# First sequence's weighted values summed by TensorE in PSUM, with new ranks for the first phase's order

## The chip, the cores and the metric

One Trainium2 chip, one core of it. The metric is the device time of one execution in microseconds (us), the median over several runs.

## What is computed

Two transformer-like layers over 32 sequences of 256 tokens, 256 wide, 16 heads of 16. The first step of the first layer is what the change is about: each token's projected vector `kx` is cut into 16 heads, and the heads of one token attend to each other.

```python
kx = modulated_linear(x, s, k_aff_w, k_aff_b, k_w, k_b)
kx = kx.reshape(B, N, H, D)                                   # 32, 256, 16, 16
q = k = v = kx
scores = jnp.einsum('bnhd,bnjd->bnhj', q, k) / math.sqrt(D)   # heads by heads, within a token
A = jax.nn.softmax(scores, axis=-1)
out = jnp.einsum('bnhj,bnjd->bnhd', A, v).reshape(B, N, F)    # weighted values
out = modulated_linear(out, s, o_aff_w, o_aff_b, o_w, o_b)
...
x = x + _L0_attn_ref(_L0_cond_ref(x, ...), ...)               # attention over tokens, cosine scores
x = x + _L0_ffn_ref(_L0_cond2_ref(x, ...), ...)               # adapter, second attention, mixture of experts
x = x + _L1_attn_ref(...); x = x + _L1_ffn_ref(...)           # second layer
```

## The kernel before

Tokens lie on the 128 partitions, so a sequence is two tiles (`t` = 0, 1) of 128 tokens by 256 values. The kernel has three phases. The first takes every sequence from its input to the router's logits of the mixture of experts; the second runs the experts; the third runs the second layer. Only the first phase is changed. It ends, in the profiled execution, with the last scores' sums on TensorE at 1622 us and the last logits at about 1633 us.

The order of the first phase's instructions is written by a planner that runs when the kernel is built (`side_by_side`, line 98). Each of the 32 sequences is a Python generator (`sequence`, line 1142) that says before each step which engine it wants and for how long the planner should reckon with it (`yield DVE, 0.7`), and then issues its instructions. At each turn the planner takes the step that can start first; among equals the lower rank goes first. The rank is the sequence's number plus a number for the stage that it is in: the table `STAGES`. A low rank of "in", for instance, lets new sequences start early. Engines then run their instructions strictly in the planned order, each waiting for its own inputs on the chip. "DVE2" is a VectorE (DVE) step that the planner keeps off GpSimd's (POOL's) time, and PER, PEC and PEH are TensorE (PE) steps in other tile modes, with a small charge for the change of mode.

Buffers are rings with turns: a generator asks for one (`get("hp", ...)`), and gives it back (`back("hp")`). The ring "hp" has three buffers of 128 x 2048 values; "mm" has three banks of PSUM; seven sequences may be under way (`lanes`).

`head_softmax_attention` (line 747) does the attention between heads of a token, on DVE, because it is a small product for each token. `kk` holds each token's 256 values twice, side by side. For the scores, DVE multiplies `kk` with shifted copies of itself (L775) and sums over the 16 values of a head (L780); ScalarE (ACT) takes the exponentials (L805 to L808); DVE sums them and takes the reciprocals (L816 to L819, into `rs`). The answers follow: for each tile `t` and each half `j0` of the 16 shifts, DVE forms 8 weighted copies (L827, 128 x 2048), then halves them three times by adding one half to the other (L835: 1024, 512 and 256 values); the two halves are added (L837) and multiplied with the reciprocals (L839). The result `o0` goes to PE, which transposes it (L292) and projects it (L304); from there come `x0T` and the queries, keys and values (L866, L312), whose norms need GpSimd's power (L262) and a product on DVE (L856) before PE can transpose them (L890) and form scores (L1019). ACT takes the exponentials (L1028), PE forms the weighted sums (L1001) and transposes them (L1049), and DVE divides (L1056, `o_n`).

A second copy of the phase, with an exact softmax, stands behind a branch and is taken only if the first pass finds sums out of bounds; with these inputs it is not.

Of the kernel before, what the change touches and what calls it, by code (L numbers as in the profile page):

```python
# [17 lines left out]
ALU = mybir.AluOpType  # L18
# [4 lines left out]
P = 128  # L23
S = 256
D = 256
H = 16
DH = 16
# [5 lines left out]
PE, DVE, ACT, POOL, SP = "PE", "DVE", "ACT", "POOL", "SP"  # L33
DMA = "DMA"
DVE2 = "DVE2"
# [62 lines left out]
def side_by_side(parts, lags):  # L98
# [84 lines left out]


STAGES = {
    "in": 1.0,
    "heads": 0.5,
    "answers of heads": 1.0,
    "out of heads": 0.0,
    "queries": 0.0,  # L190
    "queries by token": 0.0,
    "scores 1": -1.5,
    "tokens 1": 0.0,
    "out 1": -6.0,
    "x1": -0.5,
    "adapter": -2.5,
    "norm 1": 2.5,
    "queries 2": 0.0,
    "scores 2": -0.5,
    "tokens 2": 5.5,  # L200
    "out 2": 0.0,
    "norm 2": -0.5,
    "gates": -0.5,
    "values": -0.5,
    "norms of queries": 0.0,
    "answers": 1.0,
    "tokens": -4.5,
    "residual in": 0.0,
    "adapter's weights": 5.5,
    "bias": 0.5,  # L210
    "residual out": 0.0,
}


# [1 line left out]
def network(ctx: ExitStack, tc: tile.TileContext, a: dict, out: bass.AP):  # L216
    nc = tc.nc
# [19 lines left out]
    ident = cst.tile([P, P], F, name="ident")  # L237
# [86 lines left out]
    def get(r, name, shape=None, dtype=F):  # L324

        pool, own, turns = rings[r]
        yield turns
        return pool.tile(shape or own, dtype, name=name, tag=r)

    def back(r):  # L330
        return "back", rings[r][2]
# [47 lines left out]
    def condition_tables(l, w, style, demod, d2, n, at=0.0):  # L379

        yield None, at
        own = w is None
        if own:
            w = yield from get("sh", "w")
        aff = yield from get("sh", "aff", [P, D])
        yield SP, 0.5
        nc.sync.dma_start(aff, a[l + "affT"])
        yield SP, 0.5
        nc.sync.dma_start(w, a[l + "wT"].rearrange("(k p) n -> p k n", p=P))
        yield None, 3.0  # L390
        w2 = yield from get("sh", "w2")
        s2 = sm.tile([P, 2, B], F, name="s2")
        ps = yield from get("mm", "mm", [P, 2, B])
        yield PE, 0.8
        for m in range(2):
            nc.tensor.matmul(ps[:, m, :], aff[:, m * P : (m + 1) * P], condT, start=True, stop=True)
        yield ACT, 0.5
        for m in range(2):
            nc.scalar.activation(
                style[:, m, :], ps[:, m, :], AF.Identity, bias=col(l + "aff", m),  # L400
                scale=1.0 / math.sqrt(P) if l == "c" else 1.0,
            )
        yield back("mm")
        yield DVE, 0.9
        nc.vector.tensor_mul(w2, w, w)
        nc.vector.tensor_mul(s2, style, style)
        ps = yield from get("mm", "mm", [P, 2, B])
        yield PE, 1.8
        for m in range(2):
            for c in range(2):  # L410
                nc.tensor.matmul(
                    ps[:, m, :], w2[:, c, m * P : (m + 1) * P], s2[:, c, :], start=(c == 0), stop=(c == 1)
                )
        yield DVE, 0.25
        nc.vector.tensor_copy(d2, ps.rearrange("p m b -> p b m"))
        yield back("mm")
        yield back("sh")
        yield back("sh")
        if own:
            yield back("sh")  # L420
        yield from demodulation(demod, d2, 0, n)
# [45 lines left out]
    before = cst.tile([P, NSB, NT * NE], BF, name="before")  # L467
# [274 lines left out]
    def windows(kk, j0, n):  # L742

        v = kk[:, :, j0 * DH : j0 * DH + D]
        return bass.AP(v.tensor, v.offset, [v.ap[0], v.ap[1], (DH, n), (1, D)])

    def head_softmax_attention(kk, o0, b, exact):
# [21 lines left out]
        for j0 in range(0, 9, 4):  # L769
            n = min(4, 9 - j0)  # L770
            r = "hp" if n == 4 else "sh"
            w = D if n == 4 or exact else D // 2
            pr = yield from get(r, "hprod", [P, 2, n, w])
# [35 lines left out]
        rs = rhead[:, 2 * b : 2 * b + 2, :]  # L809
# [3 lines left out]
        else:  # L813
# [3 lines left out]
            nc.vector.tensor_reduce(rs2, weights(0, 8, 8, 2).rearrange("p t j h -> p t h j"), AX.X, ALU.add)  # L817
            nc.vector.tensor_add(rs, rs, rs2)
        nc.vector.reciprocal(rs, rs)  # L819
        yield "stage", "answers of heads"  # L820
        for t in range(2):
            prs = []
            for j0 in (0, 8):
                pr = yield from get("hp", "hprod2")
# [317 lines left out]
    def sequence(b, exact):  # L1142
# [8 lines left out]
        yield None, 2.5  # L1151
        yield "join", tables[b >= N0, "k"]
        yield ACT, 0.95
# [22 lines left out]
        yield "stage", "heads"  # L1176
        o0 = yield from get("sh", "o0")
        yield from head_softmax_attention(kk, o0, b, exact)
        yield back("kk")
        yield "stage", "out of heads"  # L1180
# [6 lines left out]
        yield back("sh")  # L1187
        yield "join", tables[b >= N0, "o"]
        yield "join", constants_part
# [119 lines left out]
        yield "back", lanes  # L1309

    N0 = min(B, 4)
    tables = {}
    for l in ("k", "o", "c"):
        d2 = wA.tile([P, B, 2], F, name="d2_" + l)
        n = B if l == "c" else N0
        tables[False, l] = Part(condition_tables(l, wT.get(l), sty[l], dem[l], d2, n, 300.0 if l == "c" else 0.0))
# [1123 lines left out]
```

## Time and profile before

| | |
|---|---|
| median of 3 runs | 3713.29 us (3712.82 to 3715.05) |
| profiled execution, its own time | 3708.21 us |
| its span, first to last instruction | 3706.5 us |
| mean granted TensorE clock | 0.978 |
| PE busy | 3488.0 us (94%) |
| DVE busy | 2467.3 us (67%) |
| ACT busy | 1805.9 us (49%) |
| POOL busy | 1887.7 us (51%) |

In the lines of the timeline the columns are start, duration, engine, line of the kernel, operation, output<-input, shapes, the number of instructions merged, and in brackets the engine's idle time before and what ended it. A float32 matmul appears as two records. Matmul durations overlap by a little, so sums of single records can exceed the stretch in which they ran.

### The profile page before, as it was taken

To read this page: it belongs to the slowest core of one execution; us is meant where nothing else is said; L and a number is where in the kernel's file an instruction comes from. 1 tells how busy PE (TensorE), PEld (TensorE's weight loads), DVE (VectorE), ACT (ScalarE), POOL (GpSimd) and SP (SyncE) were. 2 spreads that over 40 slices of the span, in tenths; PEclk is the share of its full clock that TensorE was granted. 3 is DMA by queue.
4 is the path that set the end of the run, shared out by engine and by line. 5 is a ranking of instruction groups with operands and counts; after the bars stand their busy time and mean duration, and the time that the engine had idled before them with its cause. 6 is when DMAs were issued, how large, how long until landed. Compare 5 with 4: busy or idle time off the path is not lost. (4 is left out here: it accounts for less than half of the span.)

```text
span 3706.5 us, 55576 instructions
## 1 busy us (share of the span) xinstructions
PE 3488.0 (94%) x22001; PEld 2564.0 (69%) x22001; DVE 2467.3 (67%) x4039; ACT 1805.9 (49%) x2790; POOL 1887.7 (51%) x1515
## 2 busy tenths in 40 slices
PE   3899999999999999969999999999998999999999
PEld 2566666666666666646666666666787888888888
DVE  7999999999999999747654540011346656565554
ACT  2677777777777777732222222222333333333333
POOL 4546555555555554426546665553024656565553
PEclk7999999999999999979999999999999999999999
DMA  1011010100100111032334334222341323233321
GB/s 64 16 34 33 31 31 31 31 31 27 29 25 28 31 31 37 25 123 69 101 83 106 97 76 91 44 37 40 131 168 43 105 93 116 94 97 97 120 94 43
DMA packets 136495, 241.44 MB, mean 65 GB/s; under 512 B 19265, under 2 KB 80897, under 8 KB 133666
## 3 DMA queue, kind: packets, MB, share of 16 engines
q0 software_dynamic: 48128, 100.77, 11.2%
q1 hardware_dynamic: 87954, 136.51, 11.1%
q8 instruction: 176, 2.88, 0.3%
q14 instruction: 93, 0.76, 0.1%
q10 hardware_dynamic: 144, 0.52, 0.0%
HBM read 187.25 MB, written 50.48 MB: 64 GB/s over the span
## 5 line engine op out<-in xcount | busy, mean ns | idle before, releaser
L1028 ACT ACTIVATE pt<-sc 128x2048 f32<-128x2048 f32 x256 | 481.5, 1881 | 108.6 <-PE sc L1019 105.7
L1633 ACT ACTIVATE hid<-bh,cols 128x512 f32<-128x512 f32 x256 | 175.3, 688 | 600.5 <-PE bh L1644 600.5
L1659 PE MATMUL by<-w,hid 128*128 128x256 f32 x2048 | 454.5, 380 | 3.2 <-DVE ysb L1665 3.2
L1644 PE MATMUL bh<-ehT,w 128*128 128x512 f32 x1024 | 451.5, 594 | 0.8 <-DVE ysb L1665 0.8
L1659 PEld LDWEIGHTS by<-w,hid 128*128 128x128 f32 x2048 | 387.7, 191 | 67.8 <-issue 14.3
L262 POOL TENSOR_TENSOR n<-n,negh 128x32 f32<-128x32 f32 x64 | 364.8, 5700 | 5.3
L1567 POOL DMA_INDIRECT rrows<-ysb,row x128 | 220.3, 1721 | 259.7 <-DMA rrows<-ysb,row 146.2
L1665 DVE TENSOR_TENSOR ysb<-by,b 128x512 f32<-128x512 f32 x64 | 44.0, 688 | 456.9 <-PE by L1659 382.7
L1644 PEld LDWEIGHTS bh<-ehT,w 128*128 128x128 f32 x1024 | 194.8, 191 | 220.8 <-issue 214.7
L256 POOL TENSOR_SCALAR rstd<-mv 128x2 f32<-128x2 f32 x160 | 62.7, 392 | 506.9 <-DVE mv L362 500.5
L835 DVE TENSOR_TENSOR hprod<-hprod 128x1024 f32<-128x1024 f32 (+2 forms) x384 | 313.3, 816 | 7.1
L1019 PE MATMUL sc<-qT,kT 32*128 32x256 f32 x4096 | 294.2, 401 | 19.4 <-ACT pt L1028 17.8
L827 DVE TENSOR_TENSOR hprod<-hex,kk 128x2048 f32<-128x2048 f32 x128 | 292.2, 2283 | 0.0
L1001 PE MATMUL av<-pt,vaug 128*32 128x256 f32 x4096 | 271.8, 385 | 5.6 <-ACT pt L1028 5.6
L1019 PEld LDWEIGHTS sc<-qT,kT 32*128 32x128 f32 x4096 | 185.4, 184 | 93.7 <-ACT pt L1028 42.7
L2269 PE MATMUL dh<-zT,w_eff 128*128 128x256 f32 x1024 | 235.9, 379 | 0.5 <-DVE zT L2246 0.5
L2283 PE MATMUL do<-w_con,gT 128*128 128x256 f32 x1024 | 230.9, 379 | 0.0
L1600 POOL DMA_INDIRECT xg<-h2buf,tok x128 | 149.3, 1167 | 156.8 <-issue 69.1
L256 POOL TENSOR_SCALAR n<-n 128x32 f32<-128x32 f32 x64 | 57.1, 892 | 300.7 <-DVE n L877 184.7
L2283 PEld LDWEIGHTS do<-w_con,gT 128*128 128x128 f32 x1024 | 192.0, 190 | 24.7
L2269 PEld LDWEIGHTS dh<-zT,w_eff 128*128 128x128 f32 x1024 | 189.9, 190 | 24.2 <-ACT cT_s L344 0.7
L1001 PEld LDWEIGHTS av<-pt,vaug 128*32 128x32 f32 x4096 | 108.0, 109 | 121.0 <-issue 54.1
(615 smaller groups left out, 7375.3 us busy)
## 6 DMA issues: line engine op xcount, KB each, us to landing
w<-in_w SPq DMA_DIRECT2D x16, 1024.0 KB, 8.2
x<-rrows SPq DMA_DIRECT2D x64, 256.0 KB, 3.1
bfw<-in_upw SPq DMA_DIRECT2D x10, 1024.0 KB, 6.9
bfw<-in_dnw SPq DMA_DIRECT2D x10, 1024.0 KB, 5.1
xT<-in_xT SPq DMA_DIRECT2D x32, 256.0 KB, 3.5
x<-in_x SPq DMA_DIRECT2D x32, 256.0 KB, 2.8
ugbb<-gtab SPq DMA_DIRECT2D x32, 256.0 KB, 3.8
h2buf<-xh SPq DMA_DIRECT2D x32, 256.0 KB, 2.5
```

The lines of the kernel that those rows point to most:

```text
L262: nc.gpsimd.tensor_tensor(o, o, negh[:p].to_broadcast([p, n]), ALU.pow)
L827: nc.vector.tensor_tensor(pr.rearrange("p j (h d) -> p j h d", d=DH), weights(t, j0, 8)[:, 0].unsqueeze(3).to_broadcast([P, 8, H, DH]), wi ...
L835: nc.vector.tensor_tensor(pr[:, :n], pr[:, :n], pr[:, n : 2 * n], ALU.add)
L1001: nc.tensor.matmul(av[32 * i : 32 * i + 32, c % 2, :], va[:, kc, 4 * c + i, :], pt[:, i, kc, :], start=(kc == 0), stop=(kc == 1),)
L1019: nc.tensor.matmul(sc[:, i, kc, :], kT[r, m, kc * P : (kc + 1) * P], qT[r, e, m, :], start=True, stop=nm is None,)
L1028: nc.scalar.activation(pt, sc, AF.Exp, scale=1.0 / math.sqrt(DH))
L1567: nc.gpsimd.indirect_dma_start(rrows[:, :], bass.IndirectOffsetOnAxis(ap=row[:, j0 + t : j0 + t + 1], axis=0), y[:, t, :], None, compute_o ...
L1633: nc.scalar.activation(o, ps, AF.Relu, bias=bcol)
L1644: nc.tensor.matmul(ps, w["w1"][:, c, f * P : (f + 1) * P], hT[c], start=(c == 0), stop=(c == 1))
L1659: nc.tensor.matmul(ps[:, t, :], hid[f // 4][:, f % 4, (t0 + t) * P : (t0 + t + 1) * P], w["w2"][:, f, :], start=(f == 0), stop=(f == 7),)
L2269: nc.tensor.matmul(ps[:, g, :], w_eff[:, c, f * P : (f + 1) * P], zT[:, c, :], start=(c == 0), stop=(c == 1))
L2283: nc.tensor.matmul(ps[:, t, :], gT[:, f, t * P : (t + 1) * P], w_con[:, f, :], start=(f == 0), stop=(f == 7))
```

## The change

For the first `NPE` = 1 sequences, in the pass that is not exact, the three halvings, the last addition and the product with the reciprocals are replaced. DVE still forms the four weighted products of 128 x 2048. PE then multiplies each of their 8 parts (128 x 256) with the identity matrix and accumulates the 16 parts of a tile in PSUM. DVE takes the sums of both tiles from PSUM in one instruction that multiplies with the reciprocals. The sums of one product run as a part of their own (`summed`), each behind the one before it, and give the "hp" buffer back. All later sequences are done as before, but the ranks in `STAGES` are other ones, so the order of all sequences' instructions on every engine differs. In the changed kernel L827, L835, L837 and L839 of the later sequences are L860, L868, L870 and L872.

```diff
 STAGES = {
-    "in": 1.0,
-    "heads": 0.5,
-    "answers of heads": 1.0,
-    "out of heads": 0.0,
-    "queries": 0.0,
+    "in": -5.5,
+    "heads": 0.0,
+    "answers of heads": 0.0,
+    "out of heads": -0.5,
+    "queries": -2.0,
     "queries by token": 0.0,
-    "scores 1": -1.5,
-    "tokens 1": 0.0,
-    "out 1": -6.0,
-    "x1": -0.5,
-    "adapter": -2.5,
-    "norm 1": 2.5,
-    "queries 2": 0.0,
-    "scores 2": -0.5,
-    "tokens 2": 5.5,
-    "out 2": 0.0,
-    "norm 2": -0.5,
-    "gates": -0.5,
-    "values": -0.5,
-    "norms of queries": 0.0,
+    "scores 1": 1.0,
+    "tokens 1": 1.0,
+    "out 1": -1.5,
+    "x1": 0.0,
+    "adapter": -4.0,
+    "norm 1": 3.0,
+    "queries 2": 4.0,
+    "scores 2": -1.0,
+    "tokens 2": 4.0,
+    "out 2": -3.0,
+    "norm 2": 0.0,
+    "gates": 0.0,
+    "values": 0.0,
+    "norms of queries": -0.5,
     "answers": 1.0,
-    "tokens": -4.5,
-    "residual in": 0.0,
-    "adapter's weights": 5.5,
-    "bias": 0.5,
-    "residual out": 0.0,
+    "tokens": -2.5,
+    "residual in": 7.0,
+    "adapter's weights": 6.0,
+    "bias": 0.0,
+    "residual out": 2.0,
 }
...
         nc.vector.reciprocal(rs, rs)
+        if not exact and b < NPE:
+
+            ps = yield from get("mm", "mm", [P, 2, D])
+
+            def summed(pr, t, j0, before):
+                if before is not None:
+                    yield "join", before
+                yield PE, 3.45
+                for n in range(8):
+                    nc.tensor.matmul(ps[:, t, :], ident, pr[:, n], start=(j0 + n == 0), stop=(j0 + n == 15))
+                yield back("hp")
+
+            last = None
+            for t in range(2):
+                for j0 in (0, 8):
+                    pr = yield from get("hp", "hprod2")
+                    yield DVE2, 2.3
+                    nc.vector.tensor_tensor(
+                        pr.rearrange("p j (h d) -> p j h d", d=DH),
+                        weights(t, j0, 8)[:, 0].unsqueeze(3).to_broadcast([P, 8, H, DH]),
+                        windows(kk, j0, 8)[:, t].rearrange("p j (h d) -> p j h d", d=DH),
+                        ALU.mult,
+                    )
+                    last = Part(summed(pr, t, j0, last))
+                    yield last
+            yield "join", last
+            yield DVE, 0.7
+            nc.vector.tensor_tensor(
+                o0.rearrange("p t (h d) -> p (t h) d", d=DH), ps.rearrange("p t (h d) -> p (t h) d", d=DH),
+                rs.rearrange("p t h -> p (t h)").unsqueeze(2).to_broadcast([P, 2 * H, DH]), ALU.mult,
+            )
+            yield back("mm")
+            return
         yield "stage", "answers of heads"
...
     N0 = min(B, 4)
+    NPE = 1
```

## The prediction

> **What bounds the kernel now.** First the page's slices, to see where which engine is short of work. Each digit covers 92.7 us.
>
> ```profile
> ## 2 busy tenths in 40 slices
> PE   3899999999999999969999999999998999999999
> DVE  7999999999999999747654540011346656565554
> PEclk7999999999999999979999999999999999999999
> ```
>
> TensorE (PE) is nearly full from the third slice to the end; only the first slice, and the gap at slice 18 where the first phase ends, are thin. VectorE (DVE) is as full as PE, but only in the first 16 slices. The change touches only that first phase, so I cut it into stretches (columns: stretch, its length, busy time of PE, weight loads, DVE, ACT, POOL, then the granted clock).
>
> ```profile
> 0.00:44.00 44.00, 16.14 (x64) 12.91 (x64) 25.19 (x29) 12.07 (x27) 26.02 (x22) 0.82 0.40 129
> 44.00:100.00 56.00, 21.67 (x72) 15.21 (x76) 53.23 (x66) 14.06 (x29) 11.95 (x4) 0.59 0.04 11
> 100.00:200.00 100.00, 83.97 (x717) 54.76 (x713) 90.89 (x131) 66.92 (x101) 49.00 (x27) 0.95 0.05 15
> 200.00:1500.00 1300.00, 1248.67 (x11252) 847.62 (x11252) 1239.01 (x1856) 1000.80 (x1486) 695.86 (x427) 1.00 0.10 31
> 1500.00:1622.00 122.00, 116.26 (x1115) 77.86 (x1112) 73.13 (x158) 89.53 (x115) 34.81 (x32) 1.00 0.08 24
> ```
>
> At 1622 us the last score work of the phase is done. PE idles 27.9 + 34.3 + 16.0 + 51.3 + 5.7 = 135.2 us on the way and works 1486.7. DVE idles only 2.8 us in 44 to 100 and 61 us in 200 to 1500. So the start is DVE's, the tail after 1500 is PE's, and in between neither leads clearly. The waits of PE in the first 200 us name the culprit of the start (columns: total, times, longest):
>
> ```profile
> PE mm L292 <- DVE o L839: 38.2, 3, 27.6
> PE mm L890 <- DVE qk L856: 17.1, 3, 9.0
> ```
>
> L839 is the last step of the first sequence's answers. The timeline shows what DVE does before it, and what PE does after it:
>
> ```profile
> 41.53 2.28 DVE L827 TENSOR_TENSOR hprod<-hex,kk 128x2048 f32<-128x2048 f32 x1
> 43.85 2.41 DVE L835 TENSOR_TENSOR hprod<-hprod 128x1024 f32<-128x1024 f32 x3
> ...
> 61.15 0.43 DVE L837 TENSOR_TENSOR o<-hprod,hprod 128x256 f32<-128x256 f32 x1
> 61.61 0.42 DVE L839 TENSOR_TENSOR o<-o,rall 128x256 f32<-128x256 f32 x1
> 63.56 3.78 PE L304 MATMUL mm<-o0T,w_owT 128*128 128x256 f32 x8 [0.56 <-ACT o0T L348]
> ```
>
> Four products of 2.28 us, each followed by three halvings (2.41 us), and two pairs of small steps (0.85 us): 20.5 us, in which PE has nothing.
>
> **The change, part by part.**
>
> *DVE's relief.* Removed: 4 x 2.41 + 2 x 0.85 = 11.3 us. Added: one eviction of 128x512 from PSUM with the reciprocal; its nearest row is L1284, the same shape out of PSUM, 0.69 us. Net 10.6 us off DVE, all within a stretch in which DVE has no slack.
>
> *PE's sums.* 32 products of 128x256. The row "PE do L2283 x16" of the chain (two records to a product) takes 3.45 us for 8 such products, so 13.8 us at full clock. They start at 43.9, after 20 us without PE work, and there the trace has the clock at 0.50: from 63.56, PE ran without a gap, and the clock stayed at 0.50 until about 69.2, 5.6 us. With 5.6 us at half speed the sums take 13.8 + 2.8 = 16.6 us; the ends are 13.8 (no cold time) and 27.6 (all cold). I take 16.6, since the sums are a gapless run like that at 63.56.
> [...]
>
> *Hand-offs.* The "hp" ring has three buffers. In the new order DVE makes pieces 1 and 2 (43.8, 46.1), then a small score group and one full product of sequence 2 that keeps the third buffer (49.3), then pieces 3 and 4. Piece 3 therefore waits for PE's first sum (8 products, 5.6 us cold and the rest warm: until 50.2), piece 4 for the second (53.6). What is queued behind them on DVE is the row sum, the first product and first halving of sequence 2; all of it slips by these two waits, 0.9 and 1.1 us. PE's fourth sum ends at 60.5, DVE is at its eviction at 60.9, and o0 is complete at 61.6: only 0.4 us before today's 62.03. The first sequence hardly gains; what gains is that DVE has by then done 8.6 us (10.6 - 2.0) of other work. Bounds: 10.6 if the ring never holds DVE, and 0 if PE stays cold (its fourth sum then ends at 71.5, DVE waits some 10 us).
>
> *Warm clock.* The transposes and the two projections behind o0 took 1.34, 3.78 and 2.78 us cold; the transposes in a warm row take 0.60 (L292 at 1497.69), the projections 1.89 each (L304 at 19.37). If PE stays warm: 3.5 us less work. Bounds 0 and 3.5; I take 3.5.
>
> *PE's idle time in 44 to 100.* Adding DVE's rows along the new order from 61.6: sequence 2's o0 is complete at 81.4, and the first sequence's second normalized queries at 91.7, against 92.5 now. PE idles about 0.5 in the sums, 2.5 at eviction and o0T, 10.4 while it waits for sequence 2's o0 (71 to 81.4), 2 in that chain, 2 before the queries' transposes and 1 after: 18.4 in place of 34.3.
>
> *The new ranks.* They move everything: the order of nearly every later instruction differs. Two counts from the order: DVE's work ahead of the last o0 falls by 17.7 us (11 of them the relief, the rest small steps put behind it, where DVE has 49 us free); and PE's work behind the last o0 grows. Before, that o0 is done at 1496.2 and PE has 119.5 us of work in the 125.8 us to 1622. The new order has there 24 more score products (24.1 us for 168: 3.4), 24 more weighted sums (3.2), 8 + 8 + 4 more projections (3.9 + 4.0 + 1.9), 24 more transposes (3.8) and 4 router products (1.0): 21 us more, so the phase ends 147 us behind the last o0.
> Activation table loads (65) and changes of PE's tile mode (916) are the same in both orders: no charge.
>
> *The sum.* PE's account: work 1486.7 + 13.8 + 2.8 - 3.5 = 1499.8; idle 27.9 + 18.4 + 16.0 + 51.3 + 5.7 = 119.3, with everything from 100 us on as now. End at 1619.1, 2.9 us earlier. DVE's account: last o0 at 1496.2 - 17.7 + 2.0 = 1480.5 if DVE idles as much as now, plus 147: 1627.5, 5.5 us later. The two contradict each other by 8.4 us: at 1480.5 PE would idle some 10 us more in the steady part than now, or, if PE idles as now, DVE some 10 us less. For DVE idling less speaks that the order has its heads some 20 us of PE work further ahead: its waits for PE, ACT and POOL in 200 to 1500, 37 us by name, have more to hide behind, and PE's 16 us of idle in 100 to 200 should shrink with sequence 2 ready 14 us sooner (I take a fifth, 3 us). So I follow PE's account, and take 5 us earlier than now: 0.15%. Behind 1622 nothing changes.
>
> The profiled execution took 3708.21 us (span 3706.5 and 1.7 around it), 5.1 below the median of 3713.29; the change carries over to the median: **3708**.
>
> **The rivals.**
>
> *A, a small gain, as summed:* -5 us, itself between -12 and +1 by the bounds above. For it: the start is DVE's with certainty. Against it: the first sequence itself hardly gains. 0.40.
>
> *B, the new order also closes waits in the steady part.* PE's named waits there are 49 us, the largest for o_n (L292, 16.7), the exponentials (L1019, 12.5) and x (L292, 8.9). A third less gives 16 more: -21, 3692. For it: the ranks were set for another beginning and the whole order is new. Against: PE is 96% busy there, and each of these waits is a chain inside one sequence. 0.20.
>
> *C, slower: the tail behind the heads decides.* If DVE keeps its idle time of now, or loses more (the ring waits recur, PE's sums stay cold), the 21 us of PE work put behind the last o0 aren't paid for. Price: +5.5 at today's DVE idle, and one more for each us that DVE idles more; at 10 more, +15, 3729. It decides as soon as DVE's waits do not shrink by 5.5 us. For it: in 1500 to 1622 PE is 95% busy, so work moved there counts in full. 0.25.
>
> *D, no effect:* DVE's lead runs into the same waits of both engines and the end stays within 2 us: 3713. For it: both engines idle 4 to 5% in the steady part, each on the other. 0.15.
>
> **How the numbers follow.** About 0.2% (7.4 us) is what a measurement of this kernel can tell from no change. Faster by more: all of B and two fifths of A (its part beyond -7.4), 0.36. Slower by more: C with 2 us or more of added DVE idle, 0.22, and 0.03 of D: 0.25. Within: 0.24 of A, 0.03 of C and 0.12 of D, 0.39. The range from 3693 to 3724 holds A and D, the nearer half of B, and C up to 5 us of added DVE idle.
>
> **What would show it.** Right: four groups of 8 matmuls from about 44 to 61, the first at clock 0.5; o0 of the first sequence at 61 to 62; o0 of the second at about 81, where it is now at 95; last o0 between 1465 and 1481; end of the scores between 1610 and 1623. Wrong: the clock stays at 0.5 through the sums, DVE waits over 4 us for "hp", or PE's idle time in 200 to 1500 moves by more than 10 us from 51, in either direction: then the ranks, and not the sums, set the result.

## The result, and the profile after

The changed kernel takes 3731.51 us (median of 5 runs, 3727.24 to 3733.99), the kernel before 3713.38 us (5 runs, 3712.82 to 3715.82) on the same chip: a ratio of 1.0047, with a 95% interval from 1.0037 to 1.0058. It is 18 us slower, where 5 us faster was forecast. The profiled execution took 3733.99 us, its span is 3731.9.

The page's slices look almost alike (each digit is now 93.3 us). PE's row has the same digits from slice 3 to slice 28, with the gap at the end of the first phase still in slice 18; only DVE's digits around it differ (5, 5, 6 in slices 17 to 19, where they were 7, 4, 7):

```profile
## 2 busy tenths in 40 slices
PE   5799999999999999969999999999888999999999
...
DVE  7999999999999999556664541001336656565554
...
PEclk8899999999999999989999999999999999999999
```

The stretches show more. Columns as before: the first pair is PE, the third pair DVE, and the number ahead of the last two is the granted clock.

```profile
0.00:44.00 44.00, 15.88 (x65) 12.81 (x66) 25.27 (x29) 12.47 (x28) 26.03 (x22) 0.81 0.40 129
44.00:100.00 56.00, 43.74 (x184) 32.73 (x188) 50.91 (x64) 23.58 (x44) 19.17 (x6) 0.88 0.05 16
100.00:200.00 100.00, 75.49 (x595) 48.54 (x591) 89.97 (x119) 55.68 (x83) 44.77 (x24) 0.86 0.05 15
200.00:1500.00 1300.00, 1244.11 (x11130) 844.39 (x11129) 1221.63 (x1834) 991.84 (x1465) 694.07 (x427) 0.99 0.09 30
1500.00:1622.00 122.00, 119.98 (x1134) 83.46 (x1133) 73.89 (x163) 93.47 (x124) 34.75 (x33) 1.00 0.08 24
1622.00:1645.00 23.00, 18.55 (x185) 11.92 (x183) 6.06 (x18) 11.06 (x12) 2.17 (x3) 1.00 0.07 25
```

The start went as promised: from 44 to 100 PE works 43.7 us in place of 21.7, at clock 0.88 in place of 0.59. Then it turns: from 100 to 200 PE does 8.5 us less than before, and the clock is 0.86 where it was 0.95. From 200 to 1500 the clock reads 0.99 and not 1.00. That looks like rounding, but it stands for 34.1 us at half clock, as is shown below.

The timeline of the start, PE and DVE:

```profile
43.77 16.01 PE L829 MATMUL mm<-hprod,ident 128*128 128x256 f32 x64 [19.64 <-DVE hprod L837]
...
49.46 2.29 DVE L837 TENSOR_TENSOR hprod<-hex,kk 128x2048 f32<-128x2048 f32 x1 [0.59 <-PE mm L829]
52.91 2.29 DVE L837 TENSOR_TENSOR hprod<-hex,kk 128x2048 f32<-128x2048 f32 x1 [1.16 <-PE mm L829]
...
59.99 0.68 DVE L847 TENSOR_TENSOR o<-mm,rall 128x512 f32<-128x512 f32 x1
```

The sums, the two waits for "hp" (0.59 and 1.16 us) and the eviction (0.68 us) stand where the prediction put them, to within 1 us.

A good mark for the end of the first phase is the small product of `okmin` behind the last scores. Its row (the two times are its first and last start), before and after:

```profile
L1350 PE MATMUL mm<-okmin,ones x2: 167/168/168, 1622.0 to 1622.0; 128*1 128x5 f32 x2
```

```profile
L1384 PE MATMUL mm<-okmin,ones x2: 166/166/167, 1642.6 to 1642.6; 128*1 128x5 f32 x2
```

So 20.6 us are lost inside the first phase. The waits of PE in the first 200 us, and then in 200 to 1500:

```profile
PE mm L829 <- DVE hprod L837: 19.6, 1, 19.6
PE mm L923 <- DVE qk L889: 13.1, 4, 5.5
```

```profile
PE mm L292 <- DVE o L872: 26.0, 17, 3.0
PE mm L312 <- DVE o_n L1089: 12.5, 12, 1.1
```

Before, the wait of the o0 transposes for DVE cost 0.2 us in all of 200 to 1500, and no steady wait of PE was longer than 1.9 us:

```profile
PE mm L292 <- DVE x L1224: 8.9, 12, 1.9
...
PE mm L292 <- DVE o L839: 0.2, 1, 0.2
```

Now there are 17 waits of the o0 transposes, up to 3.0 us; seven of PE's waits there are 2.4 us or longer. One of them, with PE and DVE side by side:

```profile
500.64 2.41 DVE L868 TENSOR_TENSOR hprod<-hprod 128x1024 f32<-128x1024 f32 x3
501.29 0.33 PE L292 MATMUL mm<-ident,o 128*128 128x128 f32 x1
503.08 0.43 DVE L870 TENSOR_TENSOR o<-hprod,hprod 128x256 f32<-128x256 f32 x1
503.54 0.42 DVE L872 TENSOR_TENSOR o<-o,rall 128x256 f32<-128x256 f32 x1
...
504.02 0.55 PE L292 MATMUL mm<-ident,o 128*128 128x128 f32 x3 [2.40 <-DVE o L872]
...
505.15 2.09 PE L1052 MATMUL sc<-qT,kT 32*128 32x256 f32 x16
```

PE has transposed the first token tile of o0 and waits while DVE halves and scales the second. The score products behind it take 2.09 us; the same 16 records took 1.15 us at 499.21. The stretches say why:

```profile
502.00:504.00 2.00, 0.00 (x0) 0.00 (x0) 1.90 (x5) 2.00 (x4) 0.00 (x0) 1.00 0.00 0
504.00:505.00 1.00, 0.98 (x7) 0.76 (x7) 1.00 (x3) 0.45 (x3) 0.30 (x1) 1.00 0.00 0
505.00:506.00 1.00, 1.00 (x11) 0.78 (x12) 1.00 (x2) 0.45 (x2) 0.97 (x1) 0.57 0.08 16
506.00:508.00 2.00, 2.00 (x20) 0.83 (x20) 2.00 (x2) 0.64 (x1) 0.00 (x0) 0.50 0.00 0
508.00:509.00 1.00, 1.00 (x14) 0.38 (x7) 1.00 (x1) 1.00 (x1) 0.00 (x0) 0.73 0.00 0
```

A wait of 2.40 us, and behind it 3.4 us at half clock. The trace's clock has eight such stretches from 200 to 1500 us, 34.1 us together; before, it has none there.

To weigh this I summed PE's time of the first phase in half-microsecond stretches: busy time times clock is work at full clock, busy time times (1 - clock) is what the slow clock cost, the rest is idle. (Work is good to some 5 us, by my estimate: of the 13.8 us of the sums only 7.5 show up.)

| first phase, us | end | work | idle | slow clock |
|---|---|---|---|---|
| before | 1622.0 | 1476.9 | 135.2 | 9.9 |
| after | 1642.6 | 1484.4 | 127.0 | 31.6 |

The difference is +7.5 work, -8.2 idle, +21.7 slow clock. By this account the clock took everything. The experiments had to say whether that is so.

### The profile page after: what moved, and what is told of

Its sections match the earlier page's. It is cut to its first block, busy times and chain, and to the rows that moved or that the text cites. A ratio compares the mean times of both kernels' runs of the same rounds, so it can differ in the third digit from the quotient of the medians.

```text
span 3731.9 us, 55605 instructions
## 1 busy us (share of the span) xinstructions
PE 3516.1 (94%) x22065; PEld 2589.2 (69%) x22065; DVE 2452.8 (66%) x4024; ACT 1810.2 (49%) x2790; POOL 1884.8 (51%) x1515
## 5 line engine op out<-in xcount | busy, mean ns | idle before, releaser
L262 POOL TENSOR_TENSOR n<-n,negh 128x32 f32<-128x32 f32 x64 | 354.3, 5536 | 5.3
L868 DVE TENSOR_TENSOR hprod<-hprod 128x1024 f32<-128x1024 f32 x372 | 328.8, 884 | 8.0
L1052 PE MATMUL sc<-qT,kT 32*128 32x256 f32 x4096 | 302.2, 410 | 17.1 <-ACT pt L1061 14.5
L860 DVE TENSOR_TENSOR hprod<-hex,kk 128x2048 f32<-128x2048 f32 x124 | 293.7, 2368 | 0.0
L256 POOL TENSOR_SCALAR n<-n 128x32 f32<-128x32 f32 x64 | 39.2, 612 | 458.2 <-DVE n L910 456.5
L2317 PEld LDWEIGHTS do<-w_con,gT 128*128 128x128 f32 x1024 | 192.3, 190 | 24.5
L780 DVE TENSOR_REDUCE hex<-hprod 128x64 f32<-128x1024 f32 (+1 forms) x192 | 166.9, 902 | 1.8
```

What stands on the lines that cost most here:

```text
L262: nc.gpsimd.tensor_tensor(o, o, negh[:p].to_broadcast([p, n]), ALU.pow)
L860: nc.vector.tensor_tensor(pr.rearrange("p j (h d) -> p j h d", d=DH), weights(t, j0, 8)[:, 0].unsqueeze(3).to_broadcast([P, 8, H, DH]), wi ...
L868: nc.vector.tensor_tensor(pr[:, :n], pr[:, :n], pr[:, n : 2 * n], ALU.add)
L1052: nc.tensor.matmul(sc[:, i, kc, :], kT[r, m, kc * P : (kc + 1) * P], qT[r, e, m, :], start=True, stop=nm is None,)
L2317: nc.tensor.matmul(ps[:, t, :], gT[:, f, t * P : (t + 1) * P], w_con[:, f, :], start=(f == 0), stop=(f == 7))
```

## The experiments

All ratios are to the kernel before on the same chip, 95% intervals in brackets.

**1. The parts alone.** The theory was that the new ranks are at fault, the rival that the sums are. First the ranks of before with the sums:

```
-    "in": -5.5, ...        # all of STAGES as in the kernel after
+    "in": 1.0, ...         # all of STAGES as in the kernel before; NPE = 1 stays
```

> The change with the ranks of before: the first sequence's sums on TensorE alone. Theory (the new ranks are at fault: TensorE meets waits of 2.4 us and more in the steady part, its clock halves after them): no such waits, no halved clock between 200 and 1480 us, and a time from 9 us below the kernel before to 3 us above it (3704 to 3716). Rival (the sums are at fault, 13.8 us of work put on an engine that bounds the phase): 8 to 15 us above the kernel before.

Measured: 3812.29 us, ratio 1.0287 [1.0273, 1.0301]. And the new ranks without the sums (`NPE = 0`):

> The new ranks without the sums: all sequences on VectorE as before. Theory (the ranks are at fault): slower than the kernel before by 15 to 30 us, with halved clock in the steady part as in the changed kernel. Rival (the sums are at fault): within 6 us of the kernel before.

Measured: 3830.61 us, ratio 1.0330 [1.0316, 1.0344]. Theory and rival both miss by far, and in the same direction. From 200 to 1500 us, first of the one and then of the other:

```profile
200.00:1500.00 1300.00, 1186.32 (x10291) 798.67 (x10294) 1170.15 (x1721) 924.96 (x1381) 639.57 (x393) 0.97 0.09 28
```

```profile
200.00:1500.00 1300.00, 1201.44 (x10535) 810.19 (x10536) 1178.10 (x1730) 942.32 (x1404) 652.44 (x400) 0.97 0.09 28
```

PE idles 114 and 99 us there in place of 51, with 16 and 18 half-clock stretches (72 and 89 us). So neither part can be priced by taking the other out: in both runs the planner wrote another order for all 32 sequences, with new waits and half-clock stretches in it. Parts have to be compared in a fixed order.

**2. The clock alone, in the order of after.** The theory now: waits of 2.4 us and more in the steady part, and the half clock behind them. Eight products of the identity with itself, which nobody reads, are put ahead of the o0 transposes of six sequences, at which PE waited 2.4 to 3.0 us (0.216 us each, an estimate: in before's trace products of twice the width follow each other after 0.432). The seventh long wait, the one that ends at 313.97, is left as it was:

```
+    WARM = {b: 8 for b in (8, 10, 14, 18, 22, 26)}
...
+        for _ in range(warm):
+            nc.tensor.matmul(ps[:, 0, :P], ident, ident, start=True, stop=True)
         transpose2(ps, x2)
```

> The changed kernel with 8 more identity products (128 columns, 1.7 us together, results overwritten) ahead of the transposes of o0 in the six sequences 8, 10, 14, 18, 22 and 26, where TensorE waits 2.4 to 3.0 us: TensorE works in the wait, and what remains of it is 0.7 to 1.3 us. Theory (the wait lets the clock halve for 3.4 or 6.8 us behind it): no halved clock at those six places, 7 to 15 us faster than the changed kernel. Rival (only the waits themselves cost): same time as the changed kernel within 3 us, or slower by up to 10 us, since 10 us of work are added.

Measured: 3716.54 us, ratio 1.0025 [1.0015, 1.0035]: 8 us faster than after (by the ratios 0.22%) with 10 us more of PE work. Its stretch, the waits at these transposes, and the end of the phase:

```profile
200.00:1500.00 1300.00, 1253.98 (x11313) 855.36 (x11312) 1225.10 (x1844) 999.92 (x1475) 693.58 (x427) 1.00 0.10 30
```

```profile
PE mm L292 <- DVE o L876: 15.0, 17, 1.2
```

```profile
L1390 PE MATMUL mm<-okmin,ones x2: 167/167/167, 1631.6 to 1631.6; 128*1 128x5 f32 x2
```

The clock is at 1.00, the six waits are 1.2 us or shorter, and the phase ends 11.0 us sooner. Two half-clock stretches are left (6.8 us), and one of them stands behind the wait that was left as it was (2.78 us, ending at 313.06; half clock from 313.7 to 317.1). ACT's exponentials of the scores, 256 in all, show that this is the steady part's doing: the 65th, 97th, 129th, 161st and 193rd come 14.5, 14.4, 16.0, 18.7 and 21.4 us later in after than in before, but 10.4, 10.3, 10.3, 10.3 and 10.3 us later in after_filled. At full clock the new order runs as fast as the old one there; it is behind from the beginning.

**3. A rank against those waits.** If they come from the place of the transposes, a later rank for them should help:

```
-    "out of heads": -0.5,
+    "out of heads": 0.5,
```

> The changed kernel with one rank changed, that of the stage out of heads from -0.5 to 0.5, so that TensorE's transposes of o0 come later in its order. Theory (the waits at these transposes and the clock behind them are the loss): fewer waits over 2 us and a time nearer to the kernel before, 5 to 20 us faster than the changed kernel. Rival (the loss is the longer tail behind the last heads): no faster than the changed kernel by more than 4 us unless the last o0 moves.

Measured: 3771.38 us, ratio 1.0169 [1.0155, 1.0183], 14 half-clock stretches. A miss: as in experiment 1, the planner wrote another order for everything.

**4. The sums alone, in the order of after.** Instructions in after's order, but the first sequence's products are halved by DVE, and the identity products are left out (the 17.7 us in the expectation are the prediction's count of all DVE work that leaves the stretch ahead of the last o0; the sums' own part is 10.6):

```
-                for n in range(8):
-                    nc.tensor.matmul(ps[:, t, :], ident, pr[:, n], ...)
+                    for n in (4, 2):
+                        nc.vector.tensor_tensor(pr[:, :n], pr[:, :n], pr[:, n : 2 * n], ALU.add)
```

> The order of instructions of the kernel after, on every engine, with one difference: the first sequence's four products are summed by VectorE's halvings again and TensorE's 64 identity products are left out; the whole computation is done. It prices the sums alone, inside the new order. Forecast's term: the halvings take some 17.7 us more of VectorE than the sums leave it (with 2 us for the scaled eviction), so if VectorE's relief at the beginning carries to the end of the first phase: 8 to 16 us slower than after (3731.5), that is 3739 to 3748. Rival (the relief is absorbed by waits later in the phase, because TensorE's late stages, and not VectorE's sum, end the phase): within 4 us of after, 3727 to 3736. Second rival (the clock: starting later shifts the half-clock stretches): anything up to 15 us either way, with a different number of half-clock stretches between 200 and 1500 us than after's 8.

Measured: 3742.47 us, ratio 1.0077 [1.0063, 1.0091].

```profile
L1389 PE MATMUL mm<-okmin,ones x2: 167/168/168, 1651.2 to 1651.2; 128*1 128x5 f32 x2
```

The phase ends 8.6 us after that of after, and the exponentials are 10.5 us late at the first and 8.5 to 8.6 from the 65th on. The clock is not the reason: it costs 30.1 us here, in seven steady half-clock stretches, against 31.6 in eight. Here DVE's relief does reach the end: 8.6 us at the mark, where the prediction's net relief was 8.6 (10.6 less 2.0 for the ring). That they agree to the tenth is chance, but the size is right.

**5. The sums in the order of before.** before's order is written out as a list and followed; the first sequence is summed by PE, and its eviction is set behind DVE's next steps for the second and third sequences, so that DVE doesn't wait for it. In a second version the other sequences stand 8 us earlier against the first.

```
-    side_by_side(parts, lags)
+    side_by_side(parts, lags, listed=ORDER)   # before's order, step by step
+    NPE = 1
```

> The kernel before with its order of steps written out as a list and followed, but the first sequence's four products summed by TensorE, and VectorE's scaled eviction set behind the next two or three VectorE steps of the second and third sequences, so that it doesn't wait. No ranks are used, nothing else moves. Theory (the sums are worth having, and what made the kernel after slower is the new order with its TensorE waits of 2.4 us and more and the half-clock stretches behind them): no more than 2 half-clock stretches in 200 to 1500 us, the second sequence's o0 10 to 15 us earlier, and a time 2 to 12 us under before, 3696 to 3706. Rival (the relief at the beginning is absorbed, since the same order waits for the same later steps): within 2 us of before, 3706 to 3710. Second rival (the small shift breaks the timing of the steady part as any change of ranks did): 10 us slower or more, with 5 or more half-clock stretches.

> As the run before it (before's order as a list, the first sequence's sums on TensorE, the eviction set back), but in the list all steps of the other sequences stand 8 us (of the plan's time) earlier against the first sequence's, for the time that the sums set free. Theory: as the run before it or better, 3692 to 3706, no more than 2 half-clock stretches in 200 to 1500 us. Rival (the relief is absorbed): 3706 to 3710. Second rival (shifting the sequences against each other makes new waits of 2.4 us and more on TensorE): slower by 10 us or more, with 5 or more half-clock stretches.

Measured: 3711.20 us, ratio 0.9997 [0.9988, 1.0006], and 3729.42 us, ratio 1.0046 [1.0032, 1.0059]. In the first, the exponentials start 4.1 us sooner than before's, and from the 21st on they are 0.3 to 2.3 us ahead, with a half-clock stretch at 236 us that before hasn't. Most of the relief is gone at once: DVE stands still for the first sequence's gate, which comes from PE and stands ahead of DVE's next halvings in this order.

```profile
70.55 0.16 DVE L1215 SCALAR_TENSOR_TENSOR gate<-mm,cols 128x2 f32<-128x2 f32 x1 [6.56 <-PE mm L1213]
```

In the second they are 12.7 us late by the ninth, with seven half-clock stretches in the first 200 us and two behind. The first rival holds for the one. The second rival's price holds for the other, though its half-clock stretches lie mostly ahead of the steady part: the relief is worth little in before's order, and shifting the sequences by hand costs as much as the change did.

**6. The cold start of before.** Its PE waits in the first 135 us filled with unread products (246 in all):

```
+        for _ in range(warm):          # 165 ahead of o0's transposes, 40 and 27
+            nc.tensor.matmul(...)      # among the queries', 14 ahead of x1's
```

> The kernel before, order and ranks unchanged, with identity products that nobody reads put into TensorE's long waits of the first 135 us: 165 ahead of the first sequence's o0 transposes (idle from 24.3 to 61.9 us), 40 and 27 ahead of its first two transposes of queries (idle 9.0 and 6.2 us), 14 ahead of its x1 transposes (idle 3.9 us). At 0.216 us each they fit into those waits. Before, the clock is at half from 28.3 to 69.3, 79.5 to 100 and 127.3 to 134.1 us. Theory of the clock: these stretches are gone, the TensorE steps in them (7.3 us busy in 62 to 70, 6.1 us in 93 to 100, 3.7 us in 127 to 135) take about half as long, and 2 to 8 us of it reach the end: 3699 to 3705. Rival (VectorE sets the pace there and hides the slow clock): 3706 to 3709. If dummy products delay what stands behind them: up to 4 us slower.

Measured: 3712.16 us, ratio 1.0000 [0.9991, 1.0009].

```profile
L1358 PE MATMUL mm<-okmin,ones x2: 167/168/168, 1618.3 to 1618.3; 128*1 128x5 f32 x2
```

No half-clock stretch is left up to 1490 us; the exponentials come some 6 us sooner from the 15th on, and the phase ends 3.7 us sooner. But the rest of the span took 2088.2 us in this profile against 2084.5 before, and in the time nothing is left. 246 products that turned 72 us of half clock into full clock gained 6 us at the best place. The rival fits: DVE, which idled only 2.8 us from 44 to 100 before, sets the pace there.

**7. All long waits filled.** Both orders with the sums, their first 200 us kept warm in the same manner; after_warm2 also fills four more waits, which after_warm left:

```
+                for _ in range(0 if t or j0 else 84):   # ahead of the first sum
+                    nc.tensor.matmul(ps[:, t, :P], ident, ident, start=True, stop=True)
...
+    # after_warm: 26 ahead of the second sequence's o0, 23 and 23 among the third's queries
+    # replay_warm: 40 and 27 among the first's queries, 14 ahead of its x1
```

> The kernel after, its order unchanged, with identity products that nobody reads both in the six steady waits of after_filled (8 each) and in the long waits of the beginning: 84 ahead of the first sum (idle 19.6 us), 26 ahead of the second sequence's o0 transposes (6.0 us), 23 and 23 ahead of the third sequence's first two transposes of queries (5.2 and 5.5 us at 157 and 163 us). In after_filled the first phase ends at 1631.6 us; slow clock cost 4.8 us of TensorE time up to 100 us and 9.8 us from 100 to 200 us. Theory (the clock is all that the new order lost): most of those 14.6 us go, the first phase ends at 1619 to 1625, and the time is 6 to 12 us under after_filled's ratio of 1.0025, so a ratio to before of 0.9990 to 1.0010. Rival (the order itself, its waits of VectorE, costs the remaining 10 us): the phase ends at 1628 to 1633, ratio 1.0015 to 1.0035.

> replay_sums_0 (the order of before as a list, the first sequence's sums on TensorE, eviction set back) with products that nobody reads in the long waits: 84 ahead of the first sum, 40 and 27 ahead of the first sequence's first two transposes of queries, 14 ahead of its x1 transposes. In replay_sums_0 the first phase ended at 1621.4 us with 11.8 us of TensorE time lost to the slow clock. Theory (the sums free VectorE, and the clock took it back): phase end 1611 to 1617, ratio to before 0.9970 to 0.9990, the quickest so far. Rival (VectorE's relief is taken up by its own later waits): phase end as before_warm's, 1617 to 1620, ratio 0.9990 to 1.0005.

> after_warm with products that nobody reads in five more of the waits behind which its clock still fell: 13 between the first sequence's first two transposes of queries (idle 3.1 us at 91 us), 9 ahead of the second sequence's transposes of keys (2.2 us at 116 us), 8 between the fourth sequence's first two o0 transposes (2.1 us at 167 us), 11 ahead of the seventh sequence's o0 transposes (2.8 us at 311 us). In after_warm the first phase ended at 1629.7 us, 11.4 us behind before_warm, with 13.1 us of TensorE time lost to the slow clock against 1.8 us there and equal idle time and work; waits of 2.0 and 2.1 us for the scores' buffers (99 and 123 us) stay unfilled. Theory (what is left of the new order's loss is the clock as well): cold loss 3 to 7 us, phase end 1620 to 1626, ratio to before 0.9990 to 1.0013. Rival (the agreement of that account is chance, the order's waits of VectorE hold the end): phase end 1628 to 1631 whatever the clock, ratio 1.0015 to 1.0030.

Measured: after_warm 3722.15 us, ratio 1.0022 [1.0013, 1.0031]; replay_warm 3711.64 us, ratio 0.9992 [0.9983, 1.0001]; after_warm2 3718.63 us, ratio 1.0014 [1.0004, 1.0023]. The ends of the first phase, of replay_warm and of after_warm2 (after_warm: 1629.7):

```profile
L1488 PE MATMUL mm<-okmin,ones x2: 167/167/167, 1617.3 to 1617.3; 128*1 128x5 f32 x2
```

```profile
L1399 PE MATMUL mm<-okmin,ones x2: 167/167/167, 1628.1 to 1628.1; 128*1 128x5 f32 x2
```

The same account, unread products counted as idle time at 0.216 us each:

| first phase, us | end | work | idle | slow clock |
|---|---|---|---|---|
| before_warm (no sums, order of before) | 1618.3 | 1479.4 | 137.3 | 1.8 |
| replay_warm (sums, order of before) | 1617.3 | 1494.1 | 120.2 | 3.2 |
| after_warm2 (sums, order of after) | 1628.1 | 1491.0 | 132.5 | 5.0 |

This decides against the first account. With the clock repaired the new order still ends 10.8 us behind the old one with the same sums, by 12.3 us more idle time, and 9.6 of these lie between 100 and 200 us (26.3 against 16.7). By the phase's end the rival was right in all three runs (after_warm2's ratio lies between its two ranges): part of the slow clock's 31.6 us had lain beside waits that came up as soon as the clock was high.

**8. The later phases.** before_warm with four long waits behind the first phase filled as well (140 products):

```
+    LATER = {"ehT": 40, "xmT": 56, "cT_t": 16, "cT_h": 28}   # ahead of the first of each
```

> before_warm with products that nobody reads in four long waits of the second phase as well: 40 ahead of the first transposes of gathered rows (9.5 us of idle), 56 ahead of the first transposes of the answer (13.0 us), 16 and 28 ahead of two transposes 180 us later (3.9 and 7.0 us). In before and before_warm the second phase took 2084.5 and 2088.2 us in one profile each, with some 90 us at half clock. Theory of the clock: 3 to 8 us faster than before_warm, ratio to before 0.9978 to 0.9992. Rival (in the second phase DMA and GpSimd set those waits, and the slow clock lies beside them): ratio 0.9993 to 1.0005.

Measured: 3711.42 us, ratio 0.9998 [0.9989, 1.0007]. Behind 1500 us the half-clock time fell from 77 to 51 us, and nothing came of it, as the rival said. What sets the pace there instead of PE's clock was not shown.

## Why the prediction was wrong

Its chain of steps, one by one.

*The beginning: right.* o0 of the first sequence at 60.7 (61.6 forecast), of the second at 79.6 (81.4), the second normalized queries at 92.0 (91.7), clock 0.5 in the sums until 47.8, DVE's waits 0.59 and 1.16 us (0.9 and 1.1). The half clock lasted 4.0 us of the sums, where 5.6 was taken from the row at 63.56. The net relief of 8.6 us was found again in experiment 4, in after's order; in before's order it came to 1.0 at most (experiments 5 and 7).

*The tail: right.* 144.6 us from the last o0 to the mark, 147 forecast. What was late is that o0: 1498.0, where 1465 to 1481 was named as a sign of being right.

*PE's account: the step that failed is "with everything from 100 us on as now".* It was used for two terms. Idle time from 100 to 200 us was taken as 16.0, or less by 3, and is 24.5: the new order lets the third sequence's transposes of queries wait for DVE's norms, 5.2 us at 157 and 5.5 us at 163. From 200 to 1500 it was 51.3 and is 55.9, nearly right as a sum, and this is the trap: the sum is nearly the same, but one third of it now comes in seven waits of 2.4 to 3.0 us, and six of these were followed by 3.4 or 6.8 us at half clock. All idle time together is 127.0 us against the 119.3 of the sum, 7.7 more; the busy time is 1515.6 against 1499.8, 15.8 more. The sum held 9.2 us for the slow clock (9.9 of before, + 2.8 - 3.5); it was 31.6. No charge was made for the clock behind 100 us beyond that of before. Nor would the prediction's sign of being wrong, idle time from 200 to 1500 us that moves by more than 10 us, have shown it: it moved by 4.6.

*DVE's account: the premise "if DVE idles as much as now" failed.* DVE idles 78 us from 200 to 1500 where it had 61. The prediction saw the two accounts contradict each other by 8.4 us and chose the better one, expecting DVE to idle less. It idled 17 more, and the sum of rival C ("+5.5 at today's DVE idle, and one more for each us that DVE idles more") then gives +22.5; the phase's end moved by 20.6. So C came out as a sum, and the range stopped at 5 us of added idle time. C's two reasons, ring waits that recur and sums that stay cold, did not come true. DVE's largest waits there are for PE, which was late in turn:

```profile
DVE x L1257 <- PE mm L312: 13.4, 13, 2.8
DVE rd L1088 <- PE mm L1082: 10.8, 18, 0.9
```

How much of this the half clock made can be read from after_filled. From 44 us to the last o0 DVE idles 72.7 us before, 92.2 after and 81.1 in after_filled, where the last o0 comes at 1487.0. So 11 of the 19.5 us went with the half clock and its waits; the others stay.

By the kernels with the clock repaired, the 20.6 us are made of three parts. The sums in a fixed order: 1617.3 - 1618.3 = -1.0. The new order at full clock: 1628.1 - 1617.3 = +10.8. The slow clock of after beyond that of before: (1642.6 - 1628.1) - (1622.0 - 1618.3) = +10.8. These are differences of single profiles; the ratios agree in size (1.0014 against 0.9992 for the order, 8 us; 1.0047 against 1.0014 for the clock, 12 us). What the unread products themselves cost is not separated from this.

*"Behind 1622 nothing changes": not quite.* The rest of the span took 2084.5 us before and 2089.3 after, and between 2083.7 and 2093.3 in the other profiles of this case. In nine of the ten profiles where it took 2088 us or more, PE stood still for 3.3 to 4.9 us in two waits next to each other, some 122 to 130 us behind the end of the last expert product; before's and after_filled's profiles have neither. The first of them takes 2.4 us in after, put down to "issue": the profile shows nothing that PE waited for. What decides when these waits come stays open; before's profiled execution, 5 us under its median, did not have them.

Left open: why the new ranks put the o0 transposes ahead of DVE's second half; and whether a table of ranks made for both the sums and the chip's clock would win. The best kernel that came out of this, replay_warm, is at 0.9992 [0.9983, 1.0001]: no gain that can be told from none.

## What to carry to other kernels

Where a planner writes the order, price the order that it writes, not the edit: here the edit was worth 8.6 us in the new order and 1.0 in the old one, and the order, with the half clock that its waits brought, cost over 20. Compare idle time by the length of its pieces and not by its sum alone, since here, with TensorE 96% busy from 200 to 1500 us, a few waits of 2.4 us and more cost nearly their own length again: behind six of them (15.4 us) lay 27.3 us at half clock, which is 13.7 us of lost work on paper, and experiment 2 got 11.0 us back with one of the six left as it was. And check a cause that an account suggests by repairing it: the clock explained 21.7 us on paper and 10.8 on the chip.

## What was not expected of the hardware

The half-clock stretches of after start on a grid: by the clock's records in its trace, those from 262.8, 314.0, 409.6 and 505.1 us lie 15, 28 and 28 times 3.413 us apart, and each of the eight lasts 3.413 us or twice that. The seven long waits differ in where they lie on that grid, counted from these starts in steps of 3.413 us. The waits that end at 313.97, 408.04, 504.02, 882.41, 1072.34 and 1263.39 us each put 1.8 to 2.8 us of idle time into one step, and the trace has half clock from the end of that step on. The wait of 2.40 us that ends at 694.02 is cut by the grid into about 1.24 and 1.16, and the clock stayed up:

```profile
692.00:694.00 2.00, 0.00 (x0) 0.00 (x0) 1.90 (x5) 2.00 (x4) 0.00 (x0) 1.00 0.00 0
694.00:697.00 3.00, 2.98 (x39) 1.90 (x39) 3.00 (x5) 1.71 (x4) 1.27 (x1) 1.00 0.03 5
697.00:700.00 3.00, 3.00 (x29) 2.12 (x25) 2.96 (x2) 3.00 (x5) 0.00 (x0) 1.00 0.00 0
```

Other places don't fit with these seven. Half clock from 1488.2 us in after follows a step with 0.99 us of idle time, in which PE also had 1.29 us of products of only 8 columns; and in before_warm a wait of 1.85 us, all in one step, left the clock at 1.00:

```profile
1486.49 1.29 PE L1335 MATMUL mm<-w_wr,hT 128*128 128x8 f32 x8 [0.93 <-ACT hT L348]
```

```profile
122.87 0.98 PE L896 MATMUL mm<-ident,qk 128*128 128x128 f32 x7 [1.85 <-DVE qk L860]
```

So idle time by the profile's records does not tell which waits were followed by half clock, and what does stays open. Against the span's start the grid lies elsewhere in each profile (0.7 us in before, 3.4 in after, 1.8 in after_warm2, of 3.413). Whether the same kernel has a different number of half-clock stretches in each run was not tested, and the spread of after's times (6.8 us in 5 runs) is no sign of it: before's 21 runs on one chip spread by 10.2.
